# Layer 2's chunk loads on GpSimd's queue, its scratch laid out by (half, channel), and the first image in whole transfers

## The chip, the cores and the metric

The kernel runs on one core of one Trainium2 chip. The metric is device time in microseconds. Three runs of the kernel before gave 2608.24, 2608.46 and 2609.03 us, so its median is 2608.46 us.

## What is computed

The input `x` has 16 images of 64 channels and 128 x 128 pixels in float32. Four residual layers follow each other, and each normalises its input over groups of two channels (per image) before its own operation:

```python
x = x + _L0_conv_ref(_gn(x), L0_conv_conv_w)              # a Gram matrix of the channels, applied to the pixels, then 1x1
x = x + _L1_conv_ref(_gn(x))                              # |Scharr x| + |Scharr y|, each channel alone
x = x + _L2_conv_ref(_gn(x), L2_conv_W, L2_conv_b)        # a quarter of the channels shifted left, a quarter right, then 3x3
x = x + _L3_conv_ref(_gn(x), L3_conv_w_bin, L3_conv_w1x1, ...)  # 3x3, 1x1, batch norm over all images, clip
```

The batch norm of layer 3 needs the sums over all images. So the last step, which scales and adds, can only start when every image has been through layer 3.

## The kernel before

The work is a pipeline of steps, each of four quarters `q`, written out in one loop at the end of `tile_kernel`. An image is cut into `NS` = 8 chunks of `R` = 8 rows for each of two halves. In each step the loop calls three stages, each on another image: `Front` (layers 0 and 1), `Layer2` and `Layer3`, which start at steps 15, 25 and 35 for image 0 and 8 steps later for each next image. `Gram` runs beside them and prepares layer 0 of a later image. What each engine does, and in which order, is the order in which this loop emits the instructions (`InOrder` keeps it). An engine's queue is worked through in that order, so an instruction that waits also holds what stands behind it. Nearly all instructions go through that helper and are shown by the profile with its line, L74; they are told apart by the tiles they read and write.

The first image. `first_gram` (L455) loads image 0 in eight pieces `x_first`, each by two transfers, one for each half of the image, into partitions 0 to 63 and 64 to 127 (L466). TensorE transposes a piece into the PSUM tile `two` ("turned"); VectorE copies the columns of the lower half into the tile `xw`, ScalarE those of the upper half (L474); and the products of `xw` with itself are summed into `pg`. Then image 1's columns `xr` are loaded in eight pieces over 128 partitions, in rows of 512 bytes, and ScalarE copies them into `xw` in turn.

The residual's scratch. `Front` keeps a chunk as 128 partitions: half `h` and channel `c`. Its method `sobel` makes the result of layer 1 in the tile `u`, and `store` (L695) writes it to a DRAM scratch `x2_d`, one for each image. The profile calls it `x_d`, as it leaves numbers out. The scratch is kept by (channel, row parity), 64 rows of one parity in a plane of `PLANE` elements. A step's store is four transfers of 64 partitions, one for each half and parity.

The chunk. `Layer2.load` (L844) reads chunk `i` back into the tile `v2` ("v" in the profile, three buffers in turn) with partitions as (parity, channel): nine rows of one parity and two more elements. Three groups of channels have different starts, since a quarter of the channels is shifted by one pixel to the left and a quarter to the right, so a chunk takes six transfers, of 16, 16 and 32 partitions for each of two parities. The last chunk reads past the end of its plane and takes twelve. All these transfers are issued by SP, at quarter 1 of the step, two steps ahead of the chunk's products:

```python
for s in range(2):
    first = j * W + at - 1 + shift
    src = x2_d[b][W + first:W + first + 2 * C * PLANE].rearrange("(c s n) -> s c n", s=2, n=PLANE)
    sp.dma_start(t[s * C + c0:s * C + c1, at:end], src[s, c0:c1, 0:end - at])
```

A step later, at quarter 1, ScalarE normalises the chunk (`v<-v,co`) with the coefficients `co2` of that image, and copies out its edges. VectorE then takes differences of rows into `d2` (tiles `d2a` and `d2b`), and POOL's queue copies `d2` from SBUF to SBUF into the tile `q2` ("q" in the profile), shifted by one element, for TensorE's products `two<-q` at quarter 1 of the next step.

POOL has few other duties: the last two or three tiny operations of each chain of coefficients (`rstd` and `coefficients`, tiles `va`, `co`, `r`), and the clearing of a border row of `xh` for each image.

SP issues nearly everything else: the loads `x` and `xr` of the input, and the stores of `u` to `x_d`, of layer 2's result (also shown as `x_d`, from the tile `x`) and of layer 3's result `y` to `y_d`. In the end phase it issues the loads and the stores of the last step.

Of the kernel before, what the change touches and what calls it, by code (L numbers as in the profile page):

```python
# [15 lines left out]
B, C, H, W = 16, 64, 128, 128  # L16
P = 128
HW = H * W
HH = H // 2
NP = H // 2  # L20
R = 8
NS = HH // R
# [20 lines left out]
PLANE = NP * W  # L43
# [67 lines left out]
def tile_kernel(ctx: ExitStack, tc: tile.TileContext, x, cw_h, w2_t, b2, wbin_t, w1_t, b1, gamma, beta, consts, out):  # L111
    nc = tc.nc
    pe, dve, act, sp, pool = (InOrder(tc, e) for e in (nc.tensor, nc.vector, nc.scalar, nc.sync, nc.gpsimd))
# [8 lines left out]
    def k(name):  # L122
        return kc[:, AT[name][0]:AT[name][1]]
# [12 lines left out]
    x2_d = [dram.tile([W + (2 * C + 1) * PLANE], F32, name=f"x2_d{b}") for b in range(B)]  # L136
# [6 lines left out]
    def halves(d, h, r0, n):  # L143

        v = d[0:C * HW].rearrange("(c r) -> c r", r=HW)
        return v[:, (h * HH + r0) * W:(h * HH + r0 + n) * W]
# [2 lines left out]

        return d.rearrange("(c j s w) -> c j s w", j=NP, s=2, w=W)[:, :, s, :]  # L150

    def planes(d, shift=0):

        return d[W + shift:W + shift + 2 * C * PLANE].rearrange("(p j w) -> p j w", j=NP, w=W)

    wpool = ctx.enter_context(tc.tile_pool(name="wpool", bufs=1))
    xin = ctx.enter_context(tc.tile_pool(name="xin", bufs=2))
# [9 lines left out]
    def sv(name, n=1):  # L167
        return small.tile([P, n], F32, tag=name, name=name)
# [27 lines left out]
    xw = wpool.tile([P, W // 2, C + 1, 2], F32, name="xw")  # L196
# [29 lines left out]
    for name in ("d2a", "d2b", "q2", "d3"):  # L226
        t = wpool.tile([P, 2, CP, W + 2], F32, name=name)
# [210 lines left out]
    def gram_product(pg, w, first, end):  # L438

        s = w % 2  # L440
        pe.matmul(
            pg[s * C:(s + 1) * C, :], xw[:, w // 2, 0:C, s], xw[:, w // 2, :, s],
            start=(w < first + 2), stop=(w >= end - 2),
        )
        last[0] = s

    def rows_to_columns(b, m, t):
        act.copy(
            xw[:, :, m * C // 8:(m + 1) * C // 8, :].rearrange("p w c t -> p c w t"),
            t.rearrange("p c (w t) -> p c w t", t=2),  # L450
        )
# [3 lines left out]
    def first_gram():  # L455

        pg = ps_g.tile([P, CP, W], F32, tag="g", name="pg_0")[:, 0, 0:C + 1]
        src = []

        t = sv("sd")  # L460
        dve.memset(t, 1.0)
        act.activation(t, t, AF.Sqrt)
        for m in range(NS):
            t = ring.tile([P, 2, CP, W], F32, tag="x3", name=f"x_first_{m}", bufs=NS + 2)
            t = t.rearrange("p a j w -> p (a j w)")
            for h in range(2):  # L466
                sp.dma_start(t[h * C:(h + 1) * C], halves(x[0].rearrange("c h w -> (c h w)"), h, m * R, R))
            src.append(t)
        for m in range(NS + 1):
            if m < NS:  # L470
                two = ps_two.tile([P, 2, CP, W], F32, tag="two", name=f"turned_{m}").rearrange("p a j w -> p (a j) w")
                for j in range(R):
                    pe.transpose(two[:, j], src[m][:, j * P:(j + 1) * P], k("I"))
                for h, copy in ((0, dve.tensor_copy), (1, act.copy)):  # L474
                    copy(xw[:, m * R:(m + 1) * R, 0:C, h], two[:, :, h * C:(h + 1) * C])
            if m > 0:
                for w in range(2 * R * (m - 1), 2 * R * m):
                    gram_product(pg, w, 0, W)
        run(Front, 0, Front.first, 0)
        live[Front, 0].load(1)  # L480

        for m in range(NS):
            t = ring.tile([P, C // 8, W], F32, tag="x3", name=f"xr_1_{m}", bufs=NS + 2)
            sp.dma_start(t, x[1].rearrange("c h w -> h c w")[:, m * C // 8:(m + 1) * C // 8, :])
            rows.append(t)
        for link, _ in enumerate(gram_chain(0, pg)):
            if link in (2, 3, 4, 5, 6):
                rows_to_columns(1, link - 2, rows[link - 2])

    class Gram:  # L490
        first, last = 2, NS + 2
# [38 lines left out]
        def load(self, m):  # L530
            t = xin.tile([P, C // 8, W], F32, tag="xr", name=f"xr_{self.b}_{m}", bufs=3)
            sp.dma_start(t, x[self.b].rearrange("c h w -> h c w")[:, m * C // 8:(m + 1) * C // 8, :])
            self.xr[m] = t
# [23 lines left out]
    class Front:  # L557
        first, last = -3, NS
# [134 lines left out]
                self.x2[i] = gx  # L693

        def store(self, i):  # L695
            d = planes(x2_d[self.b]).rearrange("(c s) j w -> c s j w", s=2)
            for h in range(2):
                for s in range(2):
                    j0 = (h * HH + i * R) // 2
                    sp.dma_start(  # L700
                        d[:, s, j0:j0 + R // 2, :],
                        self.x2[i][h * C:(h + 1) * C].rearrange("p (j s) w -> p s j w", s=2)[:, s],
                    )


    def by_parity(t):
# [129 lines left out]
    class Layer2:  # L836
        first, last = -2, NS
# [6 lines left out]
        def load(self, i):  # L844


            b = self.b
            N = (R + 1) * W + 2
            t = ring.tile([P, N], F32, tag="v2", name=f"v2_{b}_{i}", bufs=3)
            for c0, c1, shift in ((0, C // 4, 1), (C // 4, C // 2, -1), (C // 2, C, 0)):  # L850
                cut = R * W + 1 - shift
                parts = [(0, i * R, N)] if i + 1 < NS else [(0, i * R, cut), (cut, -R, N)]
                for at, j, end in parts:
                    for s in range(2):

                        first = j * W + at - 1 + shift
                        src = x2_d[b][W + first:W + first + 2 * C * PLANE].rearrange("(c s n) -> s c n", s=2, n=PLANE)
                        sp.dma_start(t[s * C + c0:s * C + c1, at:end], src[s, c0:c1, 0:end - at])
            self.v[i] = t[:, 1:N - 1].rearrange("p (j w) -> p j w", w=W)
            self.whole[i] = t  # L860

# [135 lines left out]
    class Layer3:  # L997
        first, last = -1, NS
# [95 lines left out]
    def run(stage, b, i, q):  # L1094
        if 0 <= b < B and stage.first <= i <= stage.last:
            if (stage, b) not in live:
                live[stage, b] = stage(b)
            live[stage, b].at(i, q)


    first_gram()
    pace = {}
    at = 12
# [8 lines left out]
    N = R * W  # L1112
    parts = deque((b, q) for b in range(B) if b not in AGAIN for q in range(C * HW // P // N))
# [62 lines left out]
    for step in range(starts[2][1] - 2, steps):  # L1176
        now[0] = step
        for q in range(4):
            for b in range(B):

                i = step - starts[2][1] - NS * b
# [11 lines left out]
            for b in range(1, B):  # L1193
                at, n = pace[b]
# [5 lines left out]
            first = starts[2][1]  # L1200
# [22 lines left out]
            if step >= last_one and q == 2:  # L1223

                n = 3 if step == last_one else 1 if step < last_one + NS - 2 else 0
# [13 lines left out]
            if step >= last_one - NS and q == 3:  # L1239
                n = 0  # L1240
# [156 lines left out]
```

## Time and profile before

| | |
|---|---|
| median of the three runs | 2608.46 us |
| the profiled execution's own time | 2605.62 us |
| its span, first to last instruction | 2602.5 us |
| busy: PE, DVE, ACT, POOL | 2422.0, 2086.7, 2069.7, 409.3 us |
| mean granted TensorE clock | 0.969 |
| moved by DMA | 613 MB, 236 GB/s over the span |
| transfers issued by SP to write or read the scratch of layer 2 | 512 and 864 |

The profile is one execution. An engine is busy while it executes an instruction; waiting and the issuing of transfers don't count as busy (SPq is SP's issuing). "Share" of DMA is the mean busy share of the core's 16 DMA engines. In the chain of waits each piece is what the next one waited for, with its start and its length. A group `a<-b` is named by the tile it writes and the tile it reads.

### The profile page before, as it was taken

How to read it: one execution, taken by the hardware profiler on the slowest of the kernel's cores; microseconds unless marked ns; L12 is line 12 of the kernel's file. 1: busy time of each engine (PE TensorE's matmuls, PEld its weight loads, DVE VectorE, ACT ScalarE, POOL GpSimd, SP SyncE). 2: the span in 40 equal slices, each digit the busy share in tenths (PEclk: the TensorE clock that was granted, in tenths of full speed). 3: DMA queues.
4: the chain of work that ended last, by engine and by line, in shares of the span. 5: the costliest groups of instructions: out<-in, count | busy, mean ns of one | idle time of the engine just before them, and what ended most of it. 6: DMA issues, size and time to landing. Idle time of an engine off the chain costs nothing.

```text
span 2602.5 us, 51972 instructions
## 1 busy us (share of the span) xinstructions
PE 2422.0 (93%) x18790; PEld 959.1 (37%) x18790; DVE 2086.7 (80%) x2803; ACT 2069.7 (80%) x3457; POOL 409.3 (16%) x638
## 2 busy tenths in 40 slices
PE   6578899999999999999999999999999999998883
PEld 4334433434343434343433333333433333333331
DVE  4998889999999999999999999999995334433332
ACT  4777879898989898989899888888886667655453
POOL 3332312112121111121212121211111000000000
PEclk8678899999999999999999999999999999999997
DMA  8799979898877777677879887787876878999999
GB/s 205 203 227 247 239 173 248 215 240 221 232 192 194 190 196 197 178 200 183 210 190 242 208 198 191 199 204 202 213 186 167 217 214 289 393 397 391 382 392 359
DMA packets 640927, 613.27 MB, mean 236 GB/s; under 512 B 55280, under 2 KB 535312, under 8 KB 640672
## 3 DMA queue, kind: packets, MB, share of 16 engines
q1 hardware_dynamic: 626848, 572.21, 77.8%
q0 software_dynamic: 13824, 37.75, 5.6%
q8 instruction: 149, 2.44, 0.4%
q14 instruction: 106, 0.87, 0.1%
HBM read 325.59 MB, written 247.47 MB: 220 GB/s over the span
## 4 chain that ended last, share of the span: by engine, by line
PE 47%; DMA 19%; DVE 12%; SPq 9%; ACT 8%; issue 3%; POOL 0%; DVEq 0%; ACTq 0%; POOLq 0%
PE two L74 23%; PE one L74 15%; SPq L74 9%; DVE u L74 4%; PE bank L74 3%; PE two_again L74 3%; DMA out<-end_x 2%; PE po L74 2%; DMA v<-x_d 2%; DVE e L74 2%; ACT v L74 2%; DMA xr<-in_x 2%; DVE d L74 2%; DMA x<-in_x 2%; DMA out<-xw 1%
## 5 line engine op out<-in xcount | busy, mean ns | idle before, releaser
L74 PE MATMUL two<-d,w 64*64 64x512 f32 (+2 forms) x2992 | 692.5, 593 | 0.0
L74 PE MATMUL two_again<-v_again,w 64*64 64x508 f32 (+1 forms) x2880 | 353.3, 597 | 16.1 <-ACT v_again L74 16.0
L74 PE MATMUL one<-v,w 128*64 128x508 f32 (+2 forms) x1600 | 360.3, 582 | 8.1 <-ACT c L74 7.8
L74 PEld LDWEIGHTS two<-d,w 64*64 64x64 f32 (+1 forms) x2992 | 206.7, 134 | 419.0 <-issue 409.1
L74 PE MATMUL one<-v,wi 128*64 128x508 f32 (+3 forms) x1536 | 353.7, 595 | 0.0
L74 DVE SCALAR_TENSOR_TENSOR e<-e 128x1032 f32<-128x1032 f32 (+1 forms) x256 | 313.3, 1224 | 0.0
L74 ACT ACTIVATE xh<-po,co 128x128 f32<-128x128 f32 (+1 forms) x480 | 274.6, 622 | 25.4 <-PE po L74 18.9
L74 PE MATMUL po<-x,abd 64*64 64x512 f32 (+1 forms) x1024 | 187.2, 623 | 51.7 <-ACT xh L74 45.8
L74 DVE SCALAR_TENSOR_TENSOR y<-two,c 128x1024 f32<-128x1024 f32 x128 | 156.0, 1219 | 95.8 <-ACT v L74 65.2
L74 PE MATMUL two<-q,cross 64*64 64x508 f32 (+3 forms) x944 | 215.9, 573 | 0.0
L74 PEld LDWEIGHTS two_again<-v_again,w 64*64 64x64 f32 x2880 | 134.3, 134 | 207.9 <-issue 169.0
L74 ACT ACTIVATE v<-x,co 128x1024 f32<-128x1024 f32 (+3 forms) x256 | 203.8, 846 | 0.0
L74 DVE TENSOR_TENSOR d<-v 128x1024 f32<-128x1024 f32 x128 | 156.2, 1220 | 47.0 <-ACT v L74 29.2
L74 POOL DMA_DIRECT2D q<-d2b x138 | 72.1, 526 | 722.1 <-DVE d2b L74 419.3
L74 PEld LDWEIGHTS one<-v,w 128*64 128x64 f32 x1600 | 110.6, 137 | 203.8 <-issue 162.3
L74 ACT ACTIVATE v<-v,co 128x1154 f32<-128x1154 f32 x128 | 172.1, 1344 | 16.7 <-DMA v<-x_d 13.0
L74 PE MATMUL two<-d2a,wi 128*64 128x508 f32 (+1 forms) x768 | 183.2, 589 | 0.0
L74 DVE SCALAR_TENSOR_TENSOR u<-xh 128x1170 f32<-128x1170 f32 x128 | 175.8, 1373 | 5.3 <-ACT xh L74 5.0
L74 DVE SCALAR_TENSOR_TENSOR u<-xh,co,u 128x1024 f32<-128x1024 f32 x128 | 163.7, 1279 | 14.8 <-ACT u L74 14.7
L74 POOL DMA_DIRECT2D q<-d2a x138 | 73.8, 538 | 640.7 <-issue 298.3
L74 PE MATMUL two<-d2b,wi 128*64 128x508 f32 (+3 forms) x768 | 174.1, 564 | 0.0
L74 PEld LDWEIGHTS one<-v,wi 128*64 128x64 f32 x1536 | 101.0, 138 | 194.0 <-issue 155.1
(255 smaller groups left out, 4213.4 us busy)
## 6 DMA issues: line engine op xcount, KB each, us to landing
x<-in_x SPq DMA_DIRECT2D x256, 256.0 KB
x_d<-u SPq DMA_DIRECT2D x512, 128.0 KB
x_d<-x SPq DMA_DIRECT2D x491, 128.0 KB
xr<-in_x SPq DMA_DIRECT2D x120, 512.0 KB
y_d<-y SPq DMA_DIRECT2D x352, 128.0 KB
v<-x_d SPq DMA_DIRECT2D x448, 72.1 KB
v<-x_d SPq DMA_DIRECT2D x224, 144.2 KB
end_x<-x_d SPq DMA_DIRECT2D x42, 512.0 KB
```

What stands on the lines that cost most here:

```text
L74: return self.tc.keep_in_program_order(call(*args, **kwargs))
```

## The change

Three things are changed. First, the scratch `x2_d` is now kept by (half, channel, row parity), 32 rows in a plane. A step's store is two transfers of 128 partitions, one for each parity. Second, `Layer2.load` issues its transfers on POOL's queue in place of SP's. As a plane now ends in the middle of the image, the chunk in front of that end (chunk 3) reads past the end of its plane as the last one does, so both take twelve transfers. Third, a piece of the first image is loaded by one transfer of 128 partitions, whose partitions are (channel, half) in place of (half, channel); the copies into `xw` are divided by rows in place of halves, four rows of 128 contiguous elements for VectorE and four for ScalarE.

```diff
-    def planes(d, shift=0):
-        return d[W + shift:W + shift + 2 * C * PLANE].rearrange("(p j w) -> p j w", j=NP, w=W)
+    def planes(d):
+        return d[W:W + 2 * C * PLANE].rearrange("(p s j w) -> p s j w", s=2, j=NP // 2, w=W)
...
-            for h in range(2):
-                sp.dma_start(t[h * C:(h + 1) * C], halves(x[0].rearrange("c h w -> (c h w)"), h, m * R, R))
+            sp.dma_start(t, x[0].rearrange("c (h r) w -> (c h) (r w)", h=2)[:, m * R * W:(m + 1) * R * W])
...
-                for h, copy in ((0, dve.tensor_copy), (1, act.copy)):
-                    copy(xw[:, m * R:(m + 1) * R, 0:C, h], two[:, :, h * C:(h + 1) * C])
+                for j, copy in ((0, dve.tensor_copy), (R // 2, act.copy)):
+                    copy(
+                        xw[:, m * R + j:m * R + j + R // 2, 0:C, :].rearrange("p w c t -> p w (c t)"),
+                        two[:, j:j + R // 2],
+                    )
...
-            d = planes(x2_d[self.b]).rearrange("(c s) j w -> c s j w", s=2)
-            for h in range(2):
-                for s in range(2):
-                    j0 = (h * HH + i * R) // 2
-                    sp.dma_start(
-                        d[:, s, j0:j0 + R // 2, :],
-                        self.x2[i][h * C:(h + 1) * C].rearrange("p (j s) w -> p s j w", s=2)[:, s],
-                    )
+            d = planes(x2_d[self.b])
+            for s in range(2):
+                sp.dma_start(
+                    d[:, s, i * R // 2:(i + 1) * R // 2, :],
+                    self.x2[i].rearrange("p (j s) w -> p s j w", s=2)[:, s],
+                )
...
+            size = PLANE // 2
+            h, j = divmod(i * R, NP // 2)
             for c0, c1, shift in ((0, C // 4, 1), (C // 4, C // 2, -1), (C // 2, C, 0)):
-                cut = R * W + 1 - shift
-                parts = [(0, i * R, N)] if i + 1 < NS else [(0, i * R, cut), (cut, -R, N)]
-                for at, j, end in parts:
+                cut = R * W + 1 - shift if j + R == NP // 2 else N
+                parts = [(0, cut, h * 2 * C * size + j * W - 1 + shift)]
+                if cut < N:
+                    parts.append((cut, N, (h + 1) % 2 * 2 * C * size))
+                for at, end, first in parts:
+                    src = x2_d[b][W + first:W + first + 2 * C * size].rearrange("(c s n) -> s c n", s=2, n=size)
                     for s in range(2):
-                        first = j * W + at - 1 + shift
-                        src = x2_d[b][W + first:W + first + 2 * C * PLANE].rearrange("(c s n) -> s c n", s=2, n=PLANE)
-                        sp.dma_start(t[s * C + c0:s * C + c1, at:end], src[s, c0:c1, 0:end - at])
+                        pool.dma_start(t[s * C + c0:s * C + c1, at:end], src[s, c0:c1, 0:end - at])
```

## The prediction

> **What bounds the kernel now.** I read the busy time by stretches first, because one average over the span hides stages with different limits. Columns: stretch, length, then busy us (instructions) of PE, PEld, DVE, ACT, POOL, then granted clock, DMA share, GB/s.
>
> ```profile
> 0.00:100.00 100.00, 59.90 (x774) 40.21 (x776) 60.74 (x109) 52.33 (x74) 28.98 (x43) 0.78 0.86 213
> 100.00:200.00 100.00, 66.75 (x770) 34.39 (x768) 94.94 (x140) 77.45 (x120) 33.69 (x40) 0.78 0.84 212
> 200.00:300.00 100.00, 85.88 (x816) 41.12 (x814) 87.57 (x139) 78.31 (x131) 35.67 (x51) 0.90 0.96 245
> ...
> 1000.00:1100.00 100.00, 99.13 (x770) 37.64 (x768) 96.33 (x128) 94.30 (x163) 21.37 (x32) 1.00 0.79 205
> ...
> 2180.00:2300.00 120.00, 117.44 (x1052) 46.09 (x1046) 58.74 (x61) 84.18 (x104) 0.60 (x3) 1.00 1.02 395
> ```
>
> From 400 to 2100 us PE is 96.5 to 100 busy in every hundred and DVE is close behind: idle PE sums to only about 16 us there, so hardly anything can be won. After 2180 the tail saturates the DMA engines (share 1.02, 395 GB/s), and this change touches none of its transfers. Only the first 310 us have holes. I therefore read the waits and the chain of that window.
>
> ```profile
> ACT v L74 <- DMA v<-x_d: 13.0, 4, 5.4
> ...
> 174.40 7.48 DMA xr<-in_x
> 181.89 2.91 SPq L74
> ...
> 186.09 4.24 DMA v<-x_d
> ```
>
> Between 110 and 310 us ACT waits 13.0 us for Layer 2's chunks (total, times, longest), and the chain shows why: a chunk's load stands in SP's queue behind two `xr` loads of 7.3 and 7.5 us. DVE, idle 5.2 us between 250 and 260 alone, follows ACT. The third reading is the start: the eight pieces of the first image and then the `xr` columns of image 1.
>
> ```profile
> 11.89 1.94 PE L74 MATMUL turned<-kc,x_first 128*128 128x128 f32 x8 [1.30 <-DMA x_first<-in_x]
> ...
> 34.47 1.15 ACT L74 COPY xw<-xr 128x1024 f32<-128x1024 f32 x1 [4.53 <-DMA xr<-in_x]
> 36.15 1.15 ACT L74 COPY xw<-xr 128x1024 f32<-128x1024 f32 x1 [0.53 <-DMA xr<-in_x]
> ```
>
> PE starts at 8.65 us; from 5 to 30 us the DMA share is 1.03 to 1.06 at only 214 to 250 GB/s. The `xr` pieces, 512 KB over 128 partitions in 512 B runs, then land 1.65 us apart (318 GB/s): half-partition transfers of long runs are slower than full-partition ones of short runs.
>
> [...] The trace agrees: about 234 against 318 GB/s. [...] DMA share 0.84 to 0.96 says bandwidth is nearly used up here. [...] POOL's DMA issues take 516 to 637 ns beside a DVE that is 96% busy.
>
> ```profile
> L74 POOL DMA_DIRECT2D q<-d2a x138: 516/523/637, 161.1 to 2069.3; - x138
> L74 DVE TENSOR_TENSOR u<-u x128: 1214/1219/1358, 50.8 to 1957.7; 128x1024 f32<-128x1024 f32 x128
> ```
>
> (minimum, median, maximum ns.) DVE is not stretched either, so I cost the extra issues at nothing on DVE; if they did hold it, the row's own worst, 0.14 us over its median, at each of 128 loads would be 18 us.
>
> **The change part by part.** Counts are from the built programs.
>
> *First image.* 16 issues of 256 KB become 8 of 512 KB. 4.2 MB at 234 GB/s is 17.9 us, at an assumed 350 (between `xr`'s 318 and the tail's 395, whose loads have this very shape) 12.0: 5.9 us earlier. PE caps it: a piece costs 1.08 (`turned`) + 1.23 (`pg`) us, so eight pieces from a first landing near 7.0 us put the last `turned` at 23.8 instead of 27.48, 3.7 us. Then ACT, whose five `xr` copies now end at 42.3, is released by the later of the `xr` landings (5.9 earlier) and the coefficient chain (40.8 now, 3.7 earlier). I take **4.5 us**, bounds 0 and 7. The copies into `xw` move the same 512 elements per partition, and ACT's still waits for DVE's: nothing, with 8 x 0.1 us either way as its bound.
>
> *Residual stores.* 512 issues become 256; each costs 0.62 us of SP. One place is on the chain: at 103 to 109 us eight SP issues stand between DVE's `u` and image 1's first `x` load. Two fewer stores: **1.2 us**, bounds 0 and 2. Full-partition stores may also take less DMA time: 524 KB at 318 instead of 234 GB/s is 0.6 us a step.
>
> *Chunk loads.* SP loses 864 issues of 0.42 us, 363 us in all; most of it is idle time of a queue that bounds nothing after 310. POOL gains 960, because chunk 3 now ends at a half's edge and takes 12 transfers like chunk 7: 960 x 0.52 = 499 us, so POOL goes from 409 to about 908 busy, 35%. A step costs POOL 3.1 us, twice per image 6.2. On POOL's queue they are moved past the `q2` copies, the `xh` memsets and the coefficient chains, which all stand behind a waiting load. In the first 310 us POOL reaches a load as soon as it has issued the previous `q2` copies, some 10 us before SP does now, so the waits of 2.7, 0.2 and 4.7 us go. The last, 5.4 us for image 1's chunk 0, largely stays: its third transfer waits for the landing of the store of `u` of chunk 7, and now the chain `co2` stands behind it on POOL (ACT next). Of 13.0 us I take **5.5**, bounds -2 (the chain late by POOL's 3.1 us, less the hidden part) and 13. What is late next is DVE, 272 busy of the 300 us from 100 to 400, and the DMA engines.
>
> *Steady state, 310 to 2110.* Where does a load stand against the `q2` copies behind it?
>
> ```profile
> 1049.33 3.99 SPq L74 DMA_DIRECT2D v<-x_d  x6
> 1056.23 1.11 POOL L74 DMA_DIRECT2D q<-d2a  x2 [9.05 <-issue]
> 1063.57 1.38 ACT L74 ACTIVATE v<-v,co 128x1154 f32<-128x1154 f32 x1
> ```
>
> A 6-transfer load is off POOL 3.1 us after PE frees its buffer; the `q2` copies come 6.9 us later, so they are not late. With landings of 3.1 to 3.4 us they lie 2.7 to 7 us ahead of PE's `two<-q`, which covers small delays. Cost 0, bounds +30 (the rival below) and -10 (SP's shorter queue returns `y` buffers sooner).
>
> Sum: 4.5 + 1.2 + 5.5 = 11.2 us off. The profiled execution took 2605.62 (span 2602.5 and 3.12 around it), so 2594.4 by its measure; the median shown, 2608.46, lies 2.84 above it: **2597 us**.
>
> **The rivals.**
>
> *Hidden anyway.* From 160 to 310 us the DMA share is about 0.98 of the tail's 1.02. If bandwidth is the limit, a chunk that lands sooner makes an `xr` or `x` load later, and only part of the start is left: about 4 us, 2604.5. For: that share. Against: `xr` is prefetched three pieces ahead, and ACT waits only 1.5 us for it there. "It does not do what it says" ends here too: if buffers or store landings hold the loads back, they are issued no earlier.
>
> *Slower, through the 12-transfer loads.* The built program gives POOL's transfers eight semaphores in turn: the ninth waits for the first to land. With a landing of L us, all twelve have landed 2L + 2.1 us after PE frees the buffer (4 x 0.52 between). The room above is 1063.57 - 1049.33 = 14.2 us, so it decides from L = 6.05. Against: POOL's copies land in 3.1 to 3.4 us (medians). For: in the early four-copy steps they take longer (KB each, median us to landing):
>
> ```profile
> q<-d2b POOLq DMA_DIRECT2D x10, 130.0 KB, 5.3
> ```
>
> At L = 8, 3.9 us late, of which the `q2` cover takes 2.7 to 3.2: about 1 us at each of 28 loads (two per image, 14 images), against the gain: 2608.5 - 11 + 28 = 2625.5.
>
> *More than forecast.* All 13 us of waits, the whole 7 at the start and 5 us of the steady holes: 2582.
>
> **How the numbers follow.** Forecast 0.62, hidden 0.15, slower 0.12, more 0.11. A measurement of this kernel can tell 0.2%, 5.2 us, from no change. The forecast's own range, 2591 to 2604, is nearly all beyond it; a twentieth of its chance and half of "hidden" with it fall inside, so faster 0.77, same 0.11, slower 0.12. The range 2582 to 2608 leaves out the slower rival and a little at the low end.
>
> **What would show it.** Right: `turned` ends before 25 us; the chunk wait of ACT in 110 to 310 falls under 6 us; POOL busy near 900 us with DVE's `u<-u` still at 1219 ns; 400 to 2100 us of the same length. Wrong: ACT waiting for `v<-x_d` after 310 us, or PE for `q`; POOL issues well over 0.52 us; `xr` waits that grow by what `v` gave up.

## Result and the profile after

The changed kernel takes 2603.16 us (median of 14 runs, 2600.71 to 2608.28), the kernel before 2608.11 us beside it (14 runs, 2602.98 to 2611.31): a ratio of 0.9988, 95% interval 0.998 to 0.9995, or 3.1 us less (1.3 to 5.2). (The two medians lie 4.95 us apart, near the upper end of that interval; the ratio is what I go by throughout.) A second measurement on another chip gave 0.999 (0.9982 to 0.9999). It is a real but small gain, and not the 11.2 us of the forecast. The profiled execution took 2606.93 us (span 2605.2), 3.8 above the median, and that of before 2605.62, 2.5 below its own: the two spans may not be subtracted. Single executions of one kernel differ by some 4 us either way, so what follows rests on the runs' ratios and on intervals inside the trace that repeat from one execution to the next. One run of all, of the kernel `e12` below, took 2646 us at a lower granted clock (0.924 for 0.97) and stands in no ratio.

The stretches of the changed kernel, with the columns of the prediction:

```profile
0.00:100.00 100.00, 63.66 (x820) 42.76 (x821) 64.51 (x113) 54.91 (x77) 32.68 (x47) 0.76 0.79 218
100.00:200.00 100.00, 67.79 (x743) 34.79 (x739) 93.20 (x139) 75.10 (x116) 47.24 (x71) 0.80 0.88 224
200.00:300.00 100.00, 79.18 (x795) 38.95 (x791) 88.15 (x142) 75.47 (x128) 60.46 (x94) 0.92 0.99 247
1000.00:1100.00 100.00, 99.12 (x770) 37.63 (x768) 96.41 (x132) 94.51 (x163) 43.47 (x78) 1.00 0.79 203
```

The first 100 us got fuller (PE 63.7 us busy for 59.9). The stretch from 200 to 300 got emptier (PE 79.2 for 85.9), at the same bandwidth. The steady state is what it was. So something was won at the start and lost again before 310 us. The start, by PE's and ACT's timelines (start, duration, operation, idle before and its end):

```profile
5.21 1.94 PE L74 MATMUL turned<-kc,x_first 128*128 128x128 f32 x8 [5.21 <-DMA x_first<-in_x]
...
23.81 1.09 PE L74 MATMUL turned<-kc,x_first 128*128 128x128 f32 x8
...
27.44 1.15 ACT L74 COPY xw<-xr 128x1024 f32<-128x1024 f32 x1 [1.19 <-DMA xr<-in_x]
```

PE starts at 5.21 us, where it started at 8.65, and the last `turned` ends at 24.9. The waits (total, times, longest) from 110 to 310 us:

```profile
POOL v L74 <- DMA x_d<-u: 19.0, 2, 11.8
...
ACT v L74 <- POOL co L74: 10.0, 2, 6.3
...
PE two L74 <- DMA q<-d2b: 8.3, 2, 6.5
...
ACT v L74 <- POOL edge_lower L74: 6.5, 1, 6.5
```

ACT waits 16.5 us for POOL's coefficients (`co` and `edge_lower`), where it waited 3.9 before, and PE 8.3 us for the `q2` copies, where it waited 3.8.

The line `ACT v <- DMA v<-x_d`, 13.0 us before, is gone from the list, but not all of the waiting is. ACT's normalisations of image 0's chunks 3 and 7 still wait, and so does that of image 1's chunk 0:

```profile
190.49 1.35 ACT L74 ACTIVATE v<-v,co 128x1154 f32<-128x1154 f32 x1 [4.27 <-issue]
...
249.50 1.35 ACT L74 ACTIVATE v<-v,co 128x1154 f32<-128x1154 f32 x1 [4.17 <-DMA q<-d2a]
...
266.28 1.35 ACT L74 ACTIVATE v<-v,co 128x1154 f32<-128x1154 f32 x1 [6.32 <-POOL co L74]
```

A normalisation reads no `q`. In the built program POOL's loads and copies use the same eight semaphores in turn (at 245.80 us a copy waits 1.10 us for the landing of a load), so the profile can put a wait for a load down to a copy. In the second execution of the changed kernel the first two waits have their own name: 7.9 us, two times, for `v<-x_d`. Chunks 3 and 7 are those of twelve transfers, and POOL stopped inside such a load until an earlier transfer of it has landed, here for 3.07 us ahead of the ninth:

```profile
233.60 3.92 POOL L74 DMA_DIRECT2D v<-x_d  x8
240.60 0.49 POOL L74 DMA_DIRECT2D v<-x_d  x1 [3.07 <-DMA v<-x_d]
```

A steadier yardstick is ACT's normalisation of each chunk, `v<-v,co`, of which the trace has 128. Differences of their starts, changed kernel minus before, for its two executions:

| normalisation | changed | changed, second execution |
|---|---|---|
| image 0, chunk 0 (151.7 us in before) | -3.9 | -4.6 |
| image 1, chunk 1 (283.7) | -3.0 | -6.3 |
| image 1, chunk 2 (298.4) | +2.5 | -0.7 |
| image 1, chunk 5 (353.6) | +0.1 | -3.1 |
| last (2074.6) | +1.6 | -0.7 |

Both arrive some 4 us early, both lose 5.5 or 5.6 us in one step, from image 1's chunk 1 to its chunk 2, and from 333 us to the last one they lose 1.5 and 2.4 us more. That step is the case. In the kernel before it takes 14.68 us.

### The profile page after: what moved, and what is told of

The parts are those of the page before. It is cut to its first block, busy times and chain, and to the rows that moved or that the text cites. A ratio compares the mean times of both kernels' runs of the same rounds, so it can differ in the third digit from the quotient of the medians.

```text
span 2605.2 us, 51921 instructions
## 1 busy us (share of the span) xinstructions
PE 2425.4 (93%) x18790; PEld 957.7 (37%) x18790; DVE 2087.2 (80%) x2803; ACT 2068.7 (79%) x3457; POOL 880.7 (34%) x1598
## 3 DMA queue, kind: packets, MB, share of 16 engines
q0 software_dynamic: 48640, 113.44, 16.5%
## 4 chain that ended last, share of the span: by engine, by line
PE 46%; DMA 16%; ACT 7%; DVE 7%; issue 4%; POOL 3%; SPq 2%; DVEq 0%; POOLq 0%; ACTq 0%
PE two L74 24%; PE one L74 16%; DMA v<-x_d 4%; PE bank L74 3%; DMA out<-end_x 3%; PE po L74 2%; ACT v L74 2%; DMA out<-xw 2%; DVE u L74 2%; DMA out<-end_y 2%; SPq L74 2%; DMA out<-end_xr 1%; DVE d L74 1%; POOL v L74 1%; DMA out<-xh 1%
## 5 line engine op out<-in xcount | busy, mean ns | idle before, releaser
L74 POOL DMA_DIRECT2D v<-x_d x960 | 470.9, 497 | 180.7 <-DMA x_d<-u 71.0
L74 PE MATMUL two<-d2a,wi 128*64 128x508 f32 (+1 forms) x768 | 183.1, 589 | 0.0
```

Of the source, the lines that this page charges most:

```text
L74: return self.tc.keep_in_program_order(call(*args, **kwargs))
```

## Experiments

Ratios are to the kernel before on the same chip.

**First four: one part at a time.** `e1_first` is the kernel before with the two edits in `first_gram` alone. `e2_loads_on_sp`, `e3_early_on_sp` and `e4_loads_alone` change the queue of the chunk loads:

```diff
 e2, in the changed kernel:
-                        pool.dma_start(t[s * C + c0:s * C + c1, at:end], src[s, c0:c1, 0:end - at])
+                        sp.dma_start(t[s * C + c0:s * C + c1, at:end], src[s, c0:c1, 0:end - at])
 e3, in the changed kernel:
+                        (sp if b < 2 else pool).dma_start(...)
 e4, in the kernel before:
-                        sp.dma_start(t[s * C + c0:s * C + c1, at:end], src[s, c0:c1, 0:end - at])
+                        pool.dma_start(t[s * C + c0:s * C + c1, at:end], src[s, c0:c1, 0:end - at])
```

e1_first: 

> The kernel before with only the first image's part of the change. Theory Q (POOL's one queue): the changed kernel keeps its start gain of 3.9 us until about 280 us and loses it between 280 and 333 us because coefficient operations and q2 copies stand behind the chunk loads on POOL; without loads there the gain stays: every chunk normalisation from image 1's on 3 to 4 us earlier than before, ratio about 0.9985 (2604). Rival P (phase): the loss comes from any shift of 4 us[...]; then co takes over 4 us and ACT waits for POOL near 280 to 300 us here too, ratio 1.000. Rival B (bandwidth): the DMA engines are full until 310 us, so what starts earlier waits longer for xr and x; ratio 1.000 with those waits grown by about 4 us.

e2_loads_on_sp: 

> The changed kernel with the chunk loads back on SP's queue, all else of it kept. Theory Q: start (4) and stores (about 1) stay, ACT's waits for v<-x_d between 110 and 310 us come back at about 13 us, no wait of ACT for POOL's co or edge beyond 1 us; ratio 0.998 (2603), no worse than the changed kernel. Rival P: the loss at 280 to 333 us stays, ratio 0.9995 or more. The prediction's own step (loads on POOL are worth 5.5 us): 5 us slower than the changed kernel, ratio above 1.000.

e3_early_on_sp: 

> The changed kernel with the chunk loads of images 0 and 1 on SP's queue, of images 2 to 15 on POOL's. Theory Q, with the loss in the first 333 us only: equal to e2_loads_on_sp within 1 us, about 0.998. If the loads on POOL cost or gain something in the steady state too, this one and e2_loads_on_sp differ by it: each 1 us per image is 14 us, ratio 0.005.

e4_loads_alone: 

> The kernel before with its chunk loads moved from SP's to POOL's queue and nothing else: scratch layout, four stores a step, 896 transfers of loads and the first image as before. Theory Q: ACT's 13 us of waits for v<-x_d go, but as much comes back as waits for co, edge and q2 behind the loads; net 0 to 3 us slower, ratio 1.000 to 1.001. The prediction's step: 5.5 us faster, ratio 0.998.

Measured:

| kernel | ratio (95%) | image 0, chunk 0 | image 1, chunk 5 | step at image 1's chunk 2 |
|---|---|---|---|---|
| e1_first | 0.9996 (0.9984 to 1.0008) | -4.6 | -8.5 | 14.66 |
| e2_loads_on_sp | 0.9990 (0.998 to 1.0) | -3.7 | +0.1 | 14.65 |
| e3_early_on_sp | 0.9985 (0.9973 to 0.9996) | -4.8 | -6.3 | 14.62 |
| e4_loads_alone | 0.9990 (0.998 to 1.0) | +1.5 | -1.8 | 14.88 |

The times do not separate the theories. The traces do: the start's gain reaches the first normalisation in each kernel that has it, and the bad step is in none of the four. A shift of 4 us alone does not make it (e1), which ends rival P, and loads on POOL alone do not either (e4). Where e2 loses, the loss is another one, at image 1's chunk 0, and of the old kind:

```profile
ACT v L74 <- DMA v<-x_d: 14.3, 3, 8.1
```

This is the line of its waits from 100 to 335 us; the longest, 8.1 us, is at the place where the kernel before waits 5.4, for the load that stands behind `xr` in SP's queue. e4's waits from 100 to 335 us show what moving the loads does to it: 4.9 us in place of 13.0. Its chunk 3 has six transfers, as before, and ACT does not wait for it; of the 4.9 us, 3.8 are for chunk 7.

```profile
ACT v L74 <- DMA v<-x_d: 4.9, 2, 3.8
```

**Next four: take away or double what each theory blames**, all in the changed kernel.

```diff
 e5: the chain's tail (the operations of coefficients and done that follow the powers)
-        pool.tensor_scalar(co[:, 1:2], mean, r, -1.0, op0=ALU.mult, op1=ALU.mult)
+        dve.tensor_scalar(co[:, 1:2], mean, r, -1.0, op0=ALU.mult, op1=ALU.mult)
...
-                pool.tensor_scalar_mul(edge[half], co[:, 0:2], k(half))
+                dve.tensor_scalar_mul(edge[half], co[:, 0:2], k(half))
 e6: xr of images 2 to 6
-            sp.dma_start(t, x[self.b].rearrange("c h w -> h c w")[:, m * C // 8:(m + 1) * C // 8, :])
+            sp.dma_start(t[:, 0:n], x[self.b].rearrange("c h w -> h c w")[:, m * C // 8:m * C // 8 + n, :])   # n = C // 16
 e7: for images 0 and 1, each load in two halves z of its channels
+                            pool.dma_start(t[s * C + z[0]:s * C + z[1], at:end], src[s, z[0]:z[1], 0:end - at])
 e8: in sobel
+                if b not in (1, 2):
                     dve.scalar_tensor_tensor(gy, gy, 3.0, p[:, :, 1:W + 1], op0=ALU.mult, op1=ALU.add)
```

e5_chain_on_dve: 

> The changed kernel with the tail of the coefficient chains (co's bias and edge factors, edge_lower, edge_upper) on DVE in place of POOL, so that it no longer stands behind loads and q2 copies; POOL keeps va, the powers, loads and copies. Theory Q (POOL's one queue gives the gain back): ACT's waits for POOL's co and edge (16.5 us together between 100 and 335 us in the changed kernel's profile) fall below 5 us and the time falls by 3 to 4 us against the changed kernel, ratio to before about 0.9975. Theory B (the DMA engines' bandwidth sets the length of 110 to 310 us) and theory D (DVE's work sets it): the waits go, the time stays, ratio 0.9988.

e6_xr_half: 

> The changed kernel with half the bytes of the xr loads of images 2 to 6: four of each eight channels are loaded and copied twice, so the Gram sums of those images are of other data; ACT copies in two halves. About 7 of the 47.3 MB of 110 to 310 us go, 30 us at the 237 GB/s of this stretch. Theory B: the stretch from the first to the fourteenth chunk normalisation, 185.6 us in the changed kernel's profile, falls by 10 us or more until DVE binds (161.8 busy), time about 2593, ratio 0.995. Theories Q and D: less than 3 us, ratio 0.998 to 0.999.

e7_twice_the_issues: 

> The changed kernel with every chunk load of images 0 and 1 split by channels into two transfers of half the size, same bytes and runs: 12 issues (24 for chunks 3 and 7) at 0.5 us on POOL's queue for each of 16 chunks, 3 to 6 us more of POOL per chunk, and eight semaphores in turn for them. Theory Q: what stands behind the loads on POOL gets later by as much; 3 to 8 us slower than the changed kernel, ratio 1.000 to 1.002. Theories B and D: POOL has room, within 1 us of the changed kernel, 0.9988.

e8_less_dve: 

> The changed kernel without the last of the three DVE operations that make gy, for images 1 and 2 (their Sobel is another): 16 operations of 1.22 us, 19.5 us of DVE, some 13 of it before 335 us. Theory D: the stretch to the fourteenth chunk shrinks by 8 us or more, time about 2595, ratio 0.995. Theories B and Q: under 3 us, ratio 0.998 to 0.999.

Measured: e5 1.0052 (1.0039 to 1.0065), e6 0.998 (0.9972 to 0.9987), e7 1.0089 (1.0075 to 1.0102), e8 0.997 (0.9963 to 0.9977). e6 and e8 leave out work and so compute something else.

e6: 2 us below the changed kernel by the ratios, whose intervals overlap. The stretch of 185.6 us (from the first normalisation to the one at 333.2 us in before) takes 181.6, where theory B wanted 10 us less; the second execution of the changed kernel has 183.1. So bandwidth does not set the length of this stretch. e8: 19.5 us of DVE's work gone, about 5 us of time gone, and the stretch takes 179.9, where theory D wanted 8 us less. DVE is one limit among others, not the limit. e6 and e8 still have the bad step, 20.2 and 19.3 us.

e7 is the largest effect: 120 more issues at 0.5 us, 60 us of POOL (40 of them before 340 us), put it 23 us behind before and 26 behind the changed kernel, three times the 3 to 8 us that theory Q gave. The normalisation of image 1's chunk 5 is 15.7 us behind before, and three steps later it is 23. So POOL's time is on the path in this stretch. Its waits from 100 to 360 us, in part, suggest how: DVE follows an ACT that waits for late loads and for coefficients.

```profile
DVE u L74 <- ACT u L74: 32.5, 9, 9.2
...
ACT v L74 <- DMA v<-x_d: 16.6, 4, 6.3
...
ACT v L74 <- POOL co L74: 7.6, 2, 4.8
```

e5: the bad step is gone, 13.27 us, as theory Q expected, but the step after it takes 19.2 us where before has 16.8. The whole got slower nevertheless, by an error of the experiment: in the steady state DVE now stands waiting for POOL's powers. From 500 to 2000 us:

```profile
DVE co L74 <- POOL co L74: 20.2, 38, 2.2
```

**Third: the tail on DVE only where it helps; the changed kernel again; both remedies.** `e9` takes `tail = dve if now[0] < starts[0][1] else pool` for the operations of e5, `e10` is the changed kernel unedited, and `e11` is e9 with e3's edit.

e9_chain_on_dve_early: 

> The changed kernel with the tail of the coefficient chains on DVE only before step 35, on POOL from then on. With all chains on DVE (e5) the tenth to fourteenth normalisations lost nothing (6.0 us ahead of before at the fourteenth, the changed kernel 0.1 behind), but DVE then waited 38 times, 20.2 us, for POOL's powers between 500 and 2000 us and the end was 17.5 us late. Theory Q: the stretch to 333 us as in e5, about 6 us ahead of before, nothing lost later: 4 to 6 us faster than the changed kernel, ratio 0.997 (2601 on a chip whose before is 2609). Rival: the gain of e5's stretch was that execution's luck; then as the changed kernel, 0.9988.

e10_changed_again: 

> The changed kernel as it is, a second execution of its profile. Theory Q: the same place loses again: q2 copies of image 1's second chunk issued about 3 us after the power before them, ACT waiting about 6 us for POOL's edge_lower between 280 and 305 us, and the normalisation of image 1's third chunk 4 to 6 us less ahead than that of the second. Rival (variation from run to run): no such wait, and the chunks after it 3 to 6 us ahead of before. Ratio 0.998 to 0.9995 either way.

e11_early_on_sp_and_dve: 

> Both remedies: the chunk loads of images 0 and 1 on SP's queue (e3) and the tail of the chains on DVE before step 35 (e9). Theory Q: each takes the chain from behind the loads, so together no more than the better of the two: 0.997 to 0.9985. If ACT's remaining wait of 3.7 us for co in e3 is worth its length: 3 us below e3, 0.997.

Measured: e9 0.9981 (0.9972 to 0.999), e10 0.999 (0.9982 to 0.9999), e11 0.9982 (0.9972 to 0.9993). e10 settles that the loss is no chance: the same step, 20.33 us, and the same wait of 6.1 us for `edge_lower`. In e9 the step is 13.28, but the next one is 19.4 where before has 16.8: PE waits 6.6 us for late `q2` copies at 299.6 us (6.5 in the changed kernel, no such wait there in before). In e11, whose loads of images 0 and 1 are on SP, the two steps are 13.6 and 16.7. So moving the tail is no cure. What is late is the `q2` copies in front of it, and POOL's timeline of the changed kernel shows why:

```profile
285.45 3.02 POOL L74 DMA_DIRECT2D v<-x_d  x6
...
289.35 1.44 POOL L74 TENSOR_TENSOR co<-va,kc 128x1 f32<-128x1 f32 x1
293.88 2.14 POOL L74 DMA_DIRECT2D q<-d2b  x4 [3.09 <-issue]
296.04 2.00 POOL L74 TENSOR_SCALAR co<-me,co 128x1 f32<-128x1 f32 x1
298.14 1.16 POOL L74 TENSOR_SCALAR edge_lower<-co,kc 128x2 f32<-128x2 f32 x1
```

The same place in the kernel before:

```profile
293.94 2.14 POOL L74 DMA_DIRECT2D q<-d2b  x4
296.11 0.28 POOL L74 TENSOR_SCALAR co<-me,co 128x1 f32<-128x1 f32 x1
296.48 0.31 POOL L74 TENSOR_SCALAR edge_lower<-co,kc 128x2 f32<-128x2 f32 x1
```

The queue kept its order: `co<-me,co` starts at 296.04 us, where the issue of the last copy ends (296.02). The copies' source, `d2b`, was ready at 290.4 in the changed kernel, and yet POOL idles for 3.09 us, waiting for nothing that the profile shows. (POOL's other idle times ahead of copies carry the same word, "issue", but the two of them that I compared, ahead of the 83rd transfer and in the second execution ahead of the 119th, end 0.6 us after DVE has written the source; this one ends 3.5 us after.) The second execution, e5, e6, e8 and e9 have 3.08 to 3.10 us at the same place; before, e1 and e4 have at most 0.15. DVE does not explain it: in before it runs the same operations beside these copies (from 293.30 to 297.25 us), and they go out at once, at 293.94.

**Fourth: what makes POOL idle?** In the line of the load:

```diff
 e12:
+                        (sp if b == 0 else pool).dma_start(...)
 e13:
+                        (sp if (b, i) == (1, 2) else pool).dma_start(...)
```

e12_image_0_on_sp: 

> The changed kernel with only image 0's chunk loads on SP's queue. The loss at image 1's third normalisation (5.5 and 5.7 us in two executions of the changed kernel) goes with an idle stretch of 3.09 us of POOL before the q2 copies that ends for no reason the profile shows. If the loads just ahead cause it (theory Q, local): image 1's are still on POOL, so stretch, wait for edge_lower near 6 us and loss of 4 us or more stay. If it depends on how many transfers POOL has issued before: with 60 fewer it is gone, and the loss is under 2 us. Ratio 0.998 to 0.9995 in both.

e13_one_chunk_on_sp: 

> The changed kernel with one load, image 1's chunk 2, on SP's queue: the six transfers that stand last ahead of the coefficient chain and the q2 copies at 275 to 290 us. Theory Q, local: no idle stretch of 3.09 us before the q2 copies, ACT's wait for edge_lower under 1 us, and image 1's third normalisation loses under 1 us against the second; time 0 to 4 us below the changed kernel, 0.9975 to 0.999. If it depends on how many transfers POOL has issued before, or on what DVE does: stretch and loss stay at 3 and 4 us or more. Where only this place is mended and the time stays, the stretch is given back at the next wait.

Measured: e12 0.9999 (0.9989 to 1.001), e13 0.998 (0.9973 to 0.9987). In both the idle time at the copies and the bad step are gone (14.64 and 14.60 us). For e13 the expectation had said that a pause by count would stay. That was wrongly drawn, since the six transfers taken off POOL's queue change the count too; so e13 decides nothing between the two. For e12 theory Q did not allow it: the six loads stand directly ahead as before, and the copies go out at once.

```profile
279.27 3.02 POOL L74 DMA_DIRECT2D v<-x_d  x6
...
288.71 2.13 POOL L74 DMA_DIRECT2D q<-d2b  x4 [0.16 <-issue]
```

That left the number of transfers issued before. I counted POOL's transfers in each timeline. In all ten executions counted (the changed kernel twice, e4 to e9, e12, e13), exactly 128 transfers precede the first such pause, and in the changed kernel the next seven pauses, of 2.4 to 2.9 us, follow after 121 transfers each. The same holds of e3 and e11, where the 129th transfer comes at 481.2 and 479.8 us, after 2.81 us of idle time each. The transfers' size did not move it: in e7, whose early loads are of half the size, it is the 129th as well. In e12 it has moved to 380.90 us, in front of two loads of a later chunk, where nobody waits for it. The kernel before has it too, inside a pair of copies, ahead of its 250th transfer (129 and 121; the 129th waits 18.6 us for DVE anyway); the source of both copies was ready at 1803.3 us, and the matmul of PE that the profile names (`one`) reads nothing that a copy writes:

```profile
1803.82 0.52 POOL L74 DMA_DIRECT2D q<-d2b  x1 [9.62 <-DVE d2b L74]
1807.26 0.52 POOL L74 DMA_DIRECT2D q<-d2b  x1 [2.92 <-PE one L74]
```

e12's runs do not follow its trace, and its ratio misses the range expected. The profiled execution, at 2599.2 us, ran 5.2 us ahead of before to the end, but ten of its twelve other runs took 2606 to 2612. Where they lose it no trace shows. So a trace without the bad step is not yet a faster kernel.

**Fifth: move the count, and nothing else.**

```diff
 e14, at the kernel's start:
     for t, src in ((b2_sb, b2), (b1_sb, b1), (gamma_sb, gamma), (beta_sb, beta)):
-        pool.dma_start(t, src)
+        act.dma_start(t, src)
```

e14_four_fewer: 

> The changed kernel with the four small loads of its start (two biases, gamma, beta, 3 KB in all) issued by ACT in place of POOL; nothing else moves. In the traces so far POOL idles 2.7 to 3.1 us before its 129th transfer and then every 121 transfers, whatever they are; in the changed kernel the 129th is the first of the q2 copies ahead of image 0's edge_lower, here it is the first load of image 1's chunk 3 behind it. Theory S (the stall by count, falling on that place, is what loses 5.5 us there): the stretch of 3.09 us moves to that load, ACT's wait for edge_lower falls from 6 to under 1 us, the step from image 1's second to its third normalisation loses under 1 us (5.5 and 5.7 in the changed kernel), time about 0.998 as with e13. Theory Q (the loads ahead in POOL's queue): stretch or not, the wait and the loss stay, 0.9989.

Measured: 2601.91 us against 2609.2, ratio 0.9971 (0.996 to 0.9982). POOL's timeline:

```profile
289.21 2.14 POOL L74 DMA_DIRECT2D q<-d2b  x4 [0.16 <-issue]
291.37 0.28 POOL L74 TENSOR_SCALAR co<-me,co 128x1 f32<-128x1 f32 x1
291.75 0.31 POOL L74 TENSOR_SCALAR edge_lower<-co,kc 128x2 f32<-128x2 f32 x1
...
297.53 3.98 POOL L74 DMA_DIRECT2D v<-x_d  x8 [1.98 <-ACT v L74]
```

The pause at the copies is gone; its new place, the 129th transfer, is the load at 297.53, which here waits for its buffer anyway. The next one stands where the count puts it, at 484.45 us with 2.80 us. The bad step is 14.63 us, and ACT's wait for `edge_lower` is gone; its waits for `co` are still 8.7 us and that for chunk 7 is 4.4. All loads are still on POOL, directly ahead of the chain. Theory S holds, and theory Q, in its form "the loads just ahead delay the chain", falls. Fifteen kernels fall into three groups by this step: 14.6 to 14.9 us without the pause there, 19.3 to 20.3 with it, 13.3 to 13.6 with the tail on DVE. Only e7, with its doubled loads, stands between at 17.8. e14 is 7.6 us below before (4.7 to 10.4), the lowest ratio of the kernels that leave out no work. Against the changed kernel that is 4 to 5 us less, with intervals that overlap at their edges; from e9, e11 and e13 (0.998 to 0.9982) the runs do not separate it.

The step's loss can be summed. The pause gives 2.94 us (3.09 of idle time in place of 0.15). It also pushes the tail from beside DVE's `x<-two,c` into its row of four Sobel operations in the changed kernel, of which these are the first and the last:

```profile
294.48 1.24 DVE L74 SCALAR_TENSOR_TENSOR u<-u 128x1040 f32<-128x1040 f32 x1
...
297.91 1.22 DVE L74 SCALAR_TENSOR_TENSOR e<-e 128x1024 f32<-128x1024 f32 x1
```

There the first two operations of the tail take 2.00 and 1.16 us in place of 0.28 and 0.31: 2.57 more. Together 5.51, for 5.5 measured. (In e8 the row is one operation shorter and only the first is stretched: 2.95 and 1.72 make 4.67, and its step is 4.6 us over.) The first operation of the tail took 2.00 us beside these four and 0.28 beside `x<-two,c`; what it is in the four that stretches it, no run here shows.

The step after gives a part back. Over both steps the changed kernel takes 3.5 us more than before, 3.7 in its second execution; e9, with the pause and the tail on DVE, 1.2; e14 0.5.

## Why the prediction was wrong

- **First image, 4.5 us: right at the first normalisation, not shown in the time.** It comes 3.9 and 4.6 us earlier, and 3.4 to 4.8 in the other kernels that have this edit and leave the tail on POOL. From 5 to 15 us the DMA engines move 355 and 345 GB/s, where 350 was assumed and before has 250 and 242. The cap by PE held: one `turned` follows the other in 2.18 us without a wait of PE for pieces, and the last ends at 24.9 us, 1.1 later than I put it. But e1, which has this part alone, is at 0.9996: between 4.2 us faster and 2.1 slower.
- **Residual stores, 1.2 us: not seen.** e1 and e2 differ in them, and the first normalisation of e2 is later by 0.9, not earlier; single executions and ratios (0.9996 and 0.9990) cannot resolve 1 us.
- **Chunk loads, 5.5 us: the step that failed, in both halves.** First the gain. Of the waits of 2.7, 0.2 and 4.7 us that were to go, the first two went. That for image 0's chunk 7 is still 4.2 us (4.1 in the second execution), and a new one of 4.3 us (3.9) stands at chunk 3, whose load has twelve transfers in the new layout: 8.4 and 7.9 us in all, over the 6 that I gave as the sign. Then the cost. The loads "are moved past the `q2` copies, the `xh` memsets and the coefficient chains", and I let their lateness turn this part into a loss of 2 us at most. The lateness measured 5.5 and 5.6 us in one step, 3.5 and 3.7 net of the step after. POOL's time per transfer was right: 880.7 us busy for 908, an issue 0.497 us for the 0.52 assumed. What I put at nothing is what happens to a queue as its number of transfers grows from 290 to 1250: the pause ahead of the 129th fell on the copies, and pushed the coefficients' tail into DVE's row.
- **Were the 5.5 us to be had?** Open. With the pause moved by four transfers (e14) the time is 5 us below e2, whose loads are on SP; from the two intervals I estimate 1 to 9. But at image 1's chunk 5 the trace of e14 is 5.1 us ahead of before, and those of e1 and e3, whose early loads are on SP, are 8.5 and 6.3 ahead.
- **The sum.** Of 11.2 us the changed kernel shows 3.1 (1.3 to 5.2) and e14 7.6 (4.7 to 10.4); what is left of the difference these runs do not resolve.
- **Steady state, cost 0: right.** From 353 to 2075 us the changed kernel loses 1.5 and 2.4 us in its two executions. After 310 us no normalisation waits for a load, under any name, and PE's longest wait for a copy is 0.8 us. The seven later pauses fall on transfers with room ahead, as the 6.9 us of room that I read there promised. (PE's idle time from 400 to 2100 us sums to 14.9 us, not 16; nothing hangs on it.)

```profile
L74 POOL DMA_DIRECT2D q<-d2a x138: 516/521/543, 157.2 to 2070.9; - x138
...
L74 DVE TENSOR_TENSOR u<-u x128: 1215/1220/1358, 46.9 to 1959.3; 128x1024 f32<-128x1024 f32 x128
```

- **The extra issues on POOL beside DVE: rightly costed at nothing.** The copies' issues and DVE's `u<-u` (minimum, median, maximum) moved by at most 6 ns in the median, and no maximum rose by more than 1. It is the tail's computing on POOL that was stretched (2.00 and 1.16 us for 0.28 and 0.31), which I had not looked for.
- **Rival "hidden anyway", 2604.5:** nearest to the time measured, and wrong on the reason, since taking half the `xr` bytes away changed 2 us (e6).
- **Rival "slower through the 12-transfer loads":** its condition came early, and not in the steady state where I priced it. At image 0's chunk 7 the ninth transfer went out 7.0 us after the first, once that had landed, and ACT waited for this chunk and for chunk 3. After 310 us ACT waits for none. Over the whole run loads land in a median of 3.4 us (72 KB) and 4.5 us (144 KB), below the 6.05 from which it would decide.

Open: what POOL does in the pause, where e12's other runs lose their time, what the waits for chunks 3 and 7 are worth in time, and how much of POOL's ordinary time (e7) the changed kernel pays in waits of its own.

## To carry to other kernels

When transfers are moved to an engine that computes too, price the queue and not only the issue: list what stands in order behind each moved transfer, and who waits for that. If a step loses time in front of an operation that waits for nothing, count instructions across several kernels before you blame a neighbour; an experiment that shifts the count and nothing else costs four small transfers. When a wait leaves the list, look at the instruction that waited, and at what it reads, before you call it gone. And compare intervals between the same two events, which here repeat to 0.3 us where whole runs differ by several us.

## What the hardware showed that I had not expected

- POOL paused in issuing transfers: before its 129th in each of twelve traces, and after every 121 more for the seven pauses of the changed kernel that I counted. The idle time ahead of the 129th was 3.09 us in the changed kernel, where it is a copy, and 1.90 (e4), 2.86 (e12) and 2.81 (e3 and e11) where it is a load; ahead of the seven later ones it was 2.4 to 2.9.
- POOL's small operations stretched beside some of DVE's: `co<-me,co` took 0.28 us beside `x<-two,c` in the kernel before and 2.00 us beside the row of Sobel operations in the changed one. A pair of powers (`co<-va,kc`) took 1.95 us in the kernel before and 5.91 us in the changed one, where it ended within 1 us of the last of four DVE operations in a row. Both pairs began 0.3 us ahead of these four, so the start alone does not decide it; what does is open.
- 3 KB of start-up loads on another queue moved the time by 4 to 5 us (0.9971 against 0.9988 and 0.999; the intervals overlap at their edges).
